# Mamba scan: the layer norm's affine moved into the weights, and one group in three with its B product on GpSimd

## The chip, the cores and the metric

The kernel runs on one core of one Trainium2 chip. A core has five engines that work side by side, each on its own queue of instructions: TensorE (PE, with its weight loads as PEld), VectorE (DVE), ScalarE (ACT), GpSimd (POOL) and SyncE (SP), which here issues the DMA transfers. The metric is the device time of one execution in microseconds, from the first to the last instruction; the time before is the median of three runs.

## The reference

Four layers follow one another on an image of shape (4, 96, 64, 64): a Mamba block with fusion (L0), an SSD block (L1), a second Mamba block (L2) and a ConvNeXt block (L3). The change is in the two Mamba blocks. Each runs two sublayers over the sequence of 4096 tokens of 96 channels, and a sublayer computes this:

```python
h = (seq - mu) * jax.lax.rsqrt(var + EPS) * ln_g + ln_b
xz = h @ in_w
xs, z = jnp.split(xz, 2, axis=-1)
xp = jnp.pad(xs, ((0, 0), (DCONV - 1, 0), (0, 0)))
xc = sum((conv_w[:, k] * xp[:, k:k + L, :] for k in range(DCONV))) + conv_b
xc = jax.nn.silu(xc)
dbl = xc @ xproj_w                      # dt: 6 columns, B: 16, C: 16
delta = jax.nn.softplus(dt @ dt_w + dt_b)
dA = jnp.exp(delta[..., None] * A)      # 192 channels x 16 states
dBx = delta[..., None] * Bm[:, :, None, :] * xc[..., None]
hstates = associative_scan(comb, (dA, dBx), axis=1)[1]   # h = dA * h + dBx along the tokens
y = jnp.einsum('blds,bls->bld', hstates, Cm) + Dp * xc
y = y * jax.nn.silu(z)
return y @ out_w
```

After the two sublayers a 1x1 fusion with batch statistics closes the block. All data are float32.

## The kernel before

**Tiling.** A Mamba block is worked off in steps. A step is one pair of images, one sublayer and one chunk of 512 tokens: 2 x 2 x 8 = 32 steps in a block, 64 in both. With 192 channels, 2 images and 16 states a step has 6144 rows to scan. The channels of both images lie in three tiles j of 128 partitions, and the rows of a step are split into 24 groups (three j, four q, two halves p). A group holds two halves of 128 partitions (8 channels by 16 states) by 512 tokens.

**The front of a step** (`mamba_front`) is a generator. It runs ahead, one step in advance, in small portions between the groups of the current step. It normalizes (PE for centering and variance, ACT for the rsqrt, DVE L184 for the product, GpSimd L185 for the affine with gain and bias), convolves with the input projection multiplied into the taps (L194), projects z (L204), then dt, B and C (L217), and computes delta with softplus (`softplus`, DVE L267 and L270, GpSimd L271) and du = delta * x (GpSimd L248). delta and du are written to DRAM as `dd` and `dg`, so that they can be read back spread over partitions; B and C go the same way into `bc`. The tuple `PACE` says how many portions of the front run in each of the 24 slots of a step, and `LEAD` = 4 how many slots earlier it starts.

**The life of a group** (`Scan.run`) is spread over several slots:

- `load`, four groups ahead: SyncE reads delta from `dd`, each of 8 rows repeated for 16 states, into a tile `da` (two transfers of 256 KB). A group marked `dma` also reads du from `dg` in this way, into a second tile of the same tag. The tag has six buffers.
- `decay`, two groups ahead: ACT turns `da` into exp(delta * A) (L107).
- `spread`, one group ahead. In an ordinary group PE spreads du over the states by a 0/1 matrix into the PSUM tile `bs` (L313). In a `dma` group ACT writes the exponentials into `bs` instead, and GpSimd multiplies the loaded du by B in place (L308).
- `scan`: in an ordinary group DVE multiplies `bs` by B (L335) and then runs two scans (L340); in a `dma` group it only runs the two scans. GpSimd multiplies the states by C into `hc` (L342, three buffers), and ACT keeps the last column for the next chunk (L345).
- `sums`, two groups later: PE adds the 16 states of each channel into the PSUM tile `py` (L361). At the end of a j, `close` multiplies by silu(z) on DVE (L369), and `project` and `fuse` bring the result back to 96 channels (L377, L381, L510 to L512).

So in every group one operand of DVE's scans lies in PSUM. Before the change a group is a `dma` group where q is even and p is 1, which is one group in four: 6 of 24.

**Order.** The program is written as one stream, and a scheduler orders each engine's queue at build time; on the chip every queue is worked off in order. A wait on one engine therefore holds up everything behind it in that queue. SyncE's queue holds all loads and all writes of `dd`, `dg` and `rows`.

**The weights** (`mamba_weights`) are prepared once per sublayer: the taps of the convolution are multiplied by the input projection, with the convolution's bias as a 97th row of the last tap, which meets a row of ones in `h`.

Of the kernel before, what the change touches and what calls it, by code (L numbers as in the profile page):

```python
# [18 lines left out]
F32 = mybir.dt.float32  # L19
AF = mybir.ActivationFunctionType  # L20
ALU = mybir.AluOpType
# [4 lines left out]
B, C, HH, WW = 4, 96, 64, 64  # L26
L = HH * WW
P = 128
T = 512
# [6 lines left out]
DIN = 192  # L36
# [8 lines left out]
NQU = QUART // HEIGHT  # L45
GS = 2
# [108 lines left out]
def mamba_front(tc, k, X, pools, wt, pair, c, h, made):  # L155

    nc = tc.nc  # L160
    work, psum, dram = pools
    if c == 0:
        nc.vector.memset(h[:C, :, 0:3], 0.0)
    else:
        nc.scalar.copy(h[:C, :, 0:3], h[:C, :, T : T + 3])

    def bank(name):
        return psum.tile([P, T], F32, tag="mm", name=name)

    for b in range(2):  # L170
        pc = bank("pc")[:C]
        nc.tensor.matmul(
            pc, lhsT=k.center, rhs=X[:, 2 * pair + b, ds(c * T, T)], start=True, stop=True
        )
        sq = work.tile([P, T], F32, tag="ua", name="sq")[:C]
        nc.scalar.activation(sq, pc, AF.Square)
        yield
        pv = bank("pv")[:C]
        nc.tensor.matmul(pv, lhsT=k.mean, rhs=sq, start=True, stop=True)
        rs = work.tile([P, T], F32, tag="lg", name="rs")[:C]  # L180
        rsqrt(k.act, rs, pv, k.eps[:C])
        yield
        dst = h[:C, b, 3 : 3 + T]
        nc.vector.tensor_tensor(dst, pc, rs, ALU.mult)  # L184
        nc.gpsimd.tensor_scalar(dst, dst, wt["ln"][:, 0:1], wt["ln"][:, 1:2], ALU.mult, ALU.add)  # L185


    xz = made["xz"] = work.tile([P, 6, T], F32, name="xz", bufs=2)
    for j in range(3):
        pu = bank("pu")  # L190
        for tap in range(4):
            kk = C + 1 if tap == 3 else C
            for r0, r1, d0, d1, b in SEGS[j]:
                nc.tensor.matmul(  # L194
                    pu[r0:r1], lhsT=wt["conv"][:kk, tap, d0:d1], rhs=h[:kk, b, ds(tap, T)],
                    start=(tap == 0), stop=(tap == 3),
                )
            yield
        nc.scalar.copy(xz[:, j], pu)
    k.act.other(xz[:, :3], xz[:, :3], AF.Silu)  # L200
    for j in range(3):
        pz = bank("pz")
        for r0, r1, d0, d1, b in SEGS[j]:
            nc.tensor.matmul(  # L204
                pz[r0:r1], lhsT=wt["in"][:, DIN + d0 : DIN + d1], rhs=h[:C, b, 3 : 3 + T],
                start=True, stop=True,
            )
        yield
        nc.scalar.copy(xz[:, 3 + j], pz)


    dbl = work.tile([P, T], F32, name="dbl")
    pd = bank("pd")
    for n in range(2):
        for b in range(2):
            j, r0, r1 = ROWS[b][n if b == 0 else 1 - n]
            nc.tensor.matmul(  # L217
                pd[2 * QUART * b : 2 * QUART * (b + 1)], lhsT=wt["xproj"][r0:r1, j],
                rhs=xz[r0:r1, j], start=(n == 0), stop=(n == 1),
            )  # L220
    yield
    nc.scalar.activation(dbl, pd, AF.Identity, bias=wt["one"])


    rows = dram.tile([P, T], F32, name="rows")
    nc.sync.dma_start(rows, dbl)
    bc = made["bc"] = work.tile([P, 2, 2, T], F32, name="bc", bufs=2)


    du = made["du"] = work.tile([P, 3, T], F32, name="du", bufs=2)  # L230
    for j in range(3):
        pt = bank("pt")
        for r0, r1, d0, d1, b in SEGS[j]:
            half = ds(HALFP * b, HALFP)
            nc.tensor.matmul(
                pt[r0:r1], lhsT=wt["dt"][half, d0:d1], rhs=dbl[half], start=True, stop=True,
            )
        delta = work.tile([P, T], F32, name="delta", bufs=2)
        softplus(nc, k.act, work, delta, pt)
        yield  # L240
        if j == 0:
            for b in range(2):
                for q in range(2):
                    r = HALFP * b + (QUART if q else RANK + 1)
                    nc.sync.dma_start(
                        bc[:, b, q], rows[r : r + NST, None].to_broadcast([NST, HEIGHT, T])
                    )
        nc.gpsimd.tensor_tensor(du[:, j], delta, xz[:, j], ALU.mult)  # L248
        for name, x in (("dd", delta), ("dg", du[:, j])):
            made[name, j] = dram.tile([P, T], F32, name=f"{name}{j}")  # L250
            nc.sync.dma_start(made[name, j], x)
    k.act.other(xz[:, 3:], xz[:, 3:], AF.Silu)

PACE = (1,) * 8 + (2,) + (1,) * 7 + (2,) + (1,) * 7
LEAD = 4


# [14 lines left out]
class Scan:  # L274
# [13 lines left out]
    def load(self, g):  # L288

        for name, which in (("da", "dd"), ("du", "dg")) if g["dma"] else (("da", "dd"),):  # L290
            g[name] = self.state.tile([P, GS, T], F32, tag="da", name=name, bufs=6)
            for i in range(GS):
                r = QUART * g["quarters"][i] + HEIGHT * g["q"]
                src = g["made"][which, g["j"]][r : r + HEIGHT].partition_broadcast(NST)
                self.tc.nc.sync.dma_start(g[name][:, i], src)
# [87 lines left out]
    def run(self, steps, wts, front, first):  # L383

        units = [(j, q, p) for j in range(3) for q in range(NQU) for p in range(2)]
        made = [first] + [{} for _ in steps[1:]]
        groups = [
            dict(
                pair=pair, sub=sub, c=c, wt=wts[sub], made=made[n], j=j, q=q, half=p, quarters=(p, p + 2),
                first=(q == 0 and p == 0), last=(q == NQU - 1 and p == 1),  # L390
                dma=(q % 2 == 0 and p == 1),
            )
            for n, (pair, sub, c) in enumerate(steps) for j, q, p in units
        ]
        total, each = len(groups), len(units)
        ahead = iter(())
        for n in range(-4, total + 6):
            slot = (n + LEAD) % each
            if slot == 0:
                for _ in ahead:  # L400
                    pass
                step = (n + LEAD) // each + 1
                ahead = front(step, made[step]) if step < len(steps) else iter(())

            def at(lag):
                return groups[n - lag] if 0 <= n - lag < total else None

            if (g := at(3)) and g["last"]:
                self.close(g)
            for stage, lag in (  # L410
                (self.load, -4), (self.spread, -1), (self.decay, -2), (self.scan, 0), (self.sums, 2),
            ):
                if g := at(lag):
                    stage(g)

            for lag, what in ((4, self.project), (5, self.fuse)):
                if (g := at(lag)) and g["last"] and g["j"] and (g["sub"] or lag == 4):
                    what(g, g["j"] - 1)
            for _ in range(PACE[slot] if slot < len(PACE) else 0):
                next(ahead, None)  # L420


def mamba_weights(nc, act, ident, wpool, w, sub, one7):
    wt = {"one": one7}

    def load(name, shape):
        wt[name] = wpool.tile(shape, F32, name=f"w_{name}{sub}")
        nc.sync.dma_start(wt[name], w[name][sub])

    load("ln", [C, 2])  # L430
    load("in", [C, 2 * DIN])
    conv = wt["conv"] = wpool.tile([C + 1, 4, DIN], F32, name=f"w_conv{sub}")
    nc.sync.dma_start(conv[:C], w["conv_wT"][sub].partition_broadcast(C))
    nc.sync.dma_start(conv[C : C + 1, 3], w["conv_b"][sub : sub + 1])
    nc.vector.tensor_tensor(
        conv[:C], conv[:C], wt["in"][:, None, :DIN].to_broadcast([C, 4, DIN]), ALU.mult
    )
    xp = wt["xproj"] = wpool.tile([P, 3, 2 * QUART], F32, name=f"w_xproj{sub}")
    nc.vector.memset(xp, 0.0)
    nb = RANK + 1 + NST  # L440
# [26 lines left out]
def mamba_fusion(ctx: ExitStack, tc, k, src, dst, w):  # L467

    nc = tc.nc
    one = ctx.enter_context(tc.tile_pool(name="m1", bufs=1))  # L470
# [5 lines left out]
    psum = ctx.enter_context(tc.tile_pool(name="mps", bufs=2, space=PSUM))  # L476
    dram = ctx.enter_context(tc.tile_pool(name="mdram", bufs=3, space=DRAM))

    one7 = one.tile([P, 1], F32, name="one7")
# [6 lines left out]
    h = one.tile([C + 1, 2, T + 3], F32, name="h")  # L486
# [25 lines left out]
        nc.vector.bn_stats(stats[:, b * NT + c], xs)  # L512
        nc.sync.dma_start(dst[b, :, ds(c * T, T)], xs)

    wts = [mamba_weights(nc, k.act, k.ident, one, w, 0, one7)]
    carry = one.tile([P, 3, P // HEIGHT], F32, name="carry")
    steps = [(pair, sub, c) for pair in range(B // 2) for sub in range(2) for c in range(NT)]

# [10 lines left out]
    for n, _ in enumerate(front(0, made)):  # L529
        if n % 4 == 3 and n // 4 - 1 in range(B):  # L530
            b = n // 4 - 1
            nc.vector.reduce_sum(gsum[:, b : b + 1], X[:, b], axis=AX.X)
    wts.append(mamba_weights(nc, k.act, k.ident, one, w, 1, one7))

    gpw = one.tile([C, C], F32, name="gpw")
    nc.sync.dma_start(gpw, w["gp_wT"])
# [752 lines left out]
```

## Time and profile before

| | |
|---|---|
| time, median of three | 10031.32 us (10020.4 to 10053.84) |
| profiled execution | 10010.64 us, span 10008.9 us |
| DVE, POOL, PE, ACT busy in the span | 82%, 70%, 86%, 55% |
| first to last scan of Mamba block L0 | 77 to 3044 us |
| granted TensorE clock | 0.939 of full speed on average |
| q1, the DMA queue of SyncE | 1520 MB, 54.6% of 16 engines' span |

A line of the view of groups reads: line of the kernel, engine, operation, output <- inputs with shapes, number of instructions, then busy time in us and mean ns of one, then the idle time of the engine just before them and what ended it. A line of the waits view reads: the waiting engine and instruction, what it waited for, then us in total, number of waits, longest. A line of the timeline gives start and duration in us. The windows view gives for a stretch its length, each engine's busy time and number of instructions, and then the TensorE clock, the share of time in which the 16 DMA engines were busy, and GB/s.

### The profile page before, as it was taken

How to read it: one execution, taken by the hardware profiler on the slowest of the kernel's cores; microseconds unless marked ns; L12 is line 12 of the kernel's file. 1: busy time of each engine (PE TensorE's matmuls, PEld its weight loads, DVE VectorE, ACT ScalarE, POOL GpSimd, SP SyncE). 2: the span in 40 equal slices, each digit the busy share in tenths (PEclk: the TensorE clock that was granted, in tenths of full speed). 3: DMA queues.
4: the chain of work that ended last, by engine and by line, in shares of the span. 5: the costliest groups of instructions: out<-in, count | busy, mean ns of one | idle time of the engine just before them, and what ended most of it. 6: DMA issues, size and time to landing. Idle time of an engine off the chain costs nothing. (4 is left out here: it accounts for less than half of the span.)

```text
span 10008.9 us, 110272 instructions
## 1 busy us (share of the span) xinstructions
PE 8562.4 (86%) x33120; PEld 3566.0 (36%) x33120; DVE 8200.6 (82%) x10877; ACT 5497.9 (55%) x10460; POOL 6966.5 (70%) x4600
## 2 busy tenths in 40 slices
PE   7888888888886888888888888788888888887688
PEld 1222212222214766666776676122222222221122
DVE  7999999999994666667666666799999999999787
ACT  5566666656653445445445444566666665665244
POOL 6888888888883555555555555688888888888322
PEclk9999999999997999999999999899999999999798
DMA  7777777777773223223222221777777767777442
GB/s 190 200 205 204 201 206 207 201 201 209 204 197 105 72 66 94 65 66 95 72 66 74 81 64 51 188 201 204 210 200 203 208 196 204 207 204 199 113 99 73
DMA packets 802257, 1527.53 MB, mean 153 GB/s; under 512 B 123933, under 2 KB 127161, under 8 KB 800890
## 3 DMA queue, kind: packets, MB, share of 16 engines
q1 hardware_dynamic: 801658, 1520.47, 54.6%
q8 instruction: 263, 4.31, 0.2%
q14 instruction: 336, 2.75, 0.1%
HBM read 1229.30 MB, written 155.98 MB: 138 GB/s over the span
## 5 line engine op out<-in xcount | busy, mean ns | idle before, releaser
L342 POOL TENSOR_TENSOR hc<-hs,bc 128x1024 f32<-128x1024 f32 x1536 | 3608.0, 2355 | 622.2 <-DVE hs L340 554.8
L340 DVE TENSOR_TENSOR_SCAN hs<-da,carry,bs 128x512 f32<-128x512 f32 x2016 | 2466.4, 1264 | 79.2 <-POOL du L308 1.0
L107 ACT ACTIVATE da<-da,w_a 128x512 f32<-128x512 f32 x2304 | 1616.5, 716 | 1268.5 <-DMA da<-dd 1218.7
L361 PE MATMUL py<-hc,selsum 128*32 128x512 f32 x6144 | 1801.4, 638 | 462.5 <-POOL hc L342 448.3
L313 PE MATMUL bs<-du,seldu 64*128 64x512 f32 x4608 | 1573.3, 676 | 204.2 <-DVE hs L340 194.5
L335 DVE TENSOR_TENSOR bs<-bs,bc 128x1024 f32<-128x1024 f32 x1152 | 1397.7, 1213 | 184.0 <-PE bs L313 181.6
L308 POOL TENSOR_TENSOR du<-du,bc 128x1024 f32<-128x1024 f32 x384 | 904.5, 2355 | 281.3 <-DMA du<-dg 160.5
L863 POOL TENSOR_TENSOR seg<-seg,cb 128x384 f32<-128x384 f32 x512 | 514.7, 1006 | 818.1 <-DVE cb L862 750.0
L361 PEld LDWEIGHTS py<-hc,selsum 128*32 128x32 f32 x6144 | 240.6, 110 | 1815.1 <-POOL hc L342 1118.2
L313 PEld LDWEIGHTS bs<-du,seldu 64*128 64x128 f32 x4608 | 446.0, 195 | 1196.2 <-DVE hs L340 852.1
L848 DVE TENSOR_SCALAR seg<-dr,dac 128x128 f32<-128x128 f32 x1536 | 660.4, 458 | 256.9 <-PE y L892 249.3
L194 PE MATMUL pu<-h,w_conv 96*128 96x512 f32 (+3 forms) x2048 | 834.6, 629 | 6.5 <-ACT rs L107 6.3
L340 DVE TENSOR_TENSOR_SCAN hs<-bs,carry,du 128x512 f32<-128x512 f32 x672 | 823.5, 1260 | 7.8 <-issue 5.0
L799 PE MATMUL front<-pk,sconv 128*128 128x512 f32 x1536 | 767.9, 609 | 9.2 <-ACT z L787 5.1
L915 ACT ACTIVATE y<-yz 128x192 f32<-128x192 f32 x512 | 186.0, 363 | 919.3 <-DVE yz L914 918.3
L867 POOL TENSOR_TENSOR xs<-pre,coef 128x576 f32<-128x576 f32 x512 | 598.3, 1175 | 56.2 <-ACT pre L112 31.5
L810 PE MATMUL front<-sconv,pk 128*128 128x192 f32 x3072 | 577.2, 330 | 45.3 <-DVE pre L815 36.0
L1152 DVE SCALAR_TENSOR_TENSOR acc<-pad,c_conv,acc 96x1024 f32<-96x1024 f32 x336 | 491.9, 1468 | 109.1 <-ACT acc L1143 58.0
L902 POOL TENSOR_TENSOR y<-y,xs 128x192 f32<-128x192 f32 x496 | 293.5, 592 | 412.8 <-DVE y L901 412.1
L345 ACT COPY carry<-hs 128x2 f32<-128x2 f32 x1344 | 250.7, 187 | 564.2 <-DVE hs L340 560.4
L107 ACT ACTIVATE bs<-da,w_a 128x512 f32<-128x512 f32 x768 | 522.0, 680 | 2.5 <-DMA da<-dd 0.7
L810 PEld LDWEIGHTS front<-sconv,pk 128*128 128x128 f32 x3072 | 497.4, 191 | 69.3 <-DVE pre L815 57.7
(191 smaller groups left out, 13881.2 us busy)
## 6 DMA issues: line engine op xcount, KB each, us to landing
da<-dd SPq DMA_DIRECT2D x3072, 256.0 KB
du<-dg SPq DMA_DIRECT2D x768, 256.0 KB
dr<-rows SPq DMA_DIRECT2D x256, 384.0 KB
bc<-rows SPq DMA_DIRECT2D x256, 256.0 KB
dd<-delta SPq DMA_DIRECT2D x192, 256.0 KB
dg<-du SPq DMA_DIRECT2D x192, 256.0 KB
pk<-xn SPq DMA_DIRECT2D x128, 384.0 KB
pk<-xn SPq DMA_DIRECT2D x128, 256.0 KB
```

Source lines behind the costliest of these rows:

```text
L107: self.last = self.scalar.activation(out, in_, func, **kw)
L194: nc.tensor.matmul(pu[r0:r1], lhsT=wt["conv"][:kk, tap, d0:d1], rhs=h[:kk, b, ds(tap, T)], start=(tap == 0), stop=(tap == 3),)
L308: nc.gpsimd.tensor_tensor(g["du"], g["du"], self.b_or_c(g, 0), ALU.mult)
L313: nc.tensor.matmul(g["bs"][:, i], lhsT=self.sel["du"][rows, g["half"], g["q"]], rhs=g["made"]["du"][rows, g["j"]], start=True, stop=True,)
L335: nc.vector.tensor_tensor(dbx, dbx, self.b_or_c(g, 0), ALU.mult)
L340: nc.vector.tensor_tensor_scan(hs[:, i], da[:, i], dbx[:, i], init, ALU.mult, ALU.add)
L342: nc.gpsimd.tensor_tensor(g["hc"], hs, self.b_or_c(g, 1), ALU.mult)
L361: nc.tensor.matmul(py[rows], lhsT=self.sel["sum"][:, g["q"]], rhs=g["hc"][:, i], start=(g["q"] == 0), stop=(g["q"] == NQU - 1),)
L799: nc.tensor.matmul(p, lhsT=self.conv[:, i, DI + q * DST : DI + (q + 1) * DST], rhs=pk[:, i, ds(c * T, T)], start=(i == 0), stop=(i == 2),)
L810: nc.tensor.matmul(p, lhsT=pk[:, i, ds(c * Q, Q)], rhs=self.conv[:, i, :DI], start=(i == 0), stop=(i == 2),)
L848: nc.vector.tensor_scalar(seg[:, h], g["pair"]["dr"][:, c % 2 * NH + h], made["dac"][:, n0 + h : n0 + h + 1], 0.0, ALU.subtract, ALU.min,)
L867: nc.gpsimd.tensor_tensor(xs, x.to_broadcast([P, 3, NH, HD]), coef.to_broadcast([P, 3, NH, HD]), ALU.mult)
```

## The change

It has three parts that belong together.

First, the affine of the layer norm is folded into the weights. The gain multiplies the rows of the convolution's and z's weights. The bias becomes a 97th row of every tap and of z: a small matmul of a matrix `shift`, whose last column is the layer norm's bias, with the weights gives this row at the start. `h` has a row of ones, which now is part of every matmul; it is zeroed, like the channels, in the three columns of padding before the first token. GpSimd's L185 is no longer needed.

Second, the groups whose index in the step is 1 modulo 3 are `dma` groups, 8 of 24. In these du comes by DMA and its product with B is on GpSimd, not on PE and DVE. The tag `da` gets seven buffers in place of six.

Third, `PACE` runs one portion of the front in each of the 24 slots. It had two portions in slots 8 and 16, so that the front was through two slots before the step's end.

```diff
     if c == 0:
-        nc.vector.memset(h[:C, :, 0:3], 0.0)
+        nc.vector.memset(h[:, :, 0:3], 0.0)
     else:
-        nc.scalar.copy(h[:C, :, 0:3], h[:C, :, T : T + 3])
+        nc.scalar.copy(h[:, :, 0:3], h[:, :, T : T + 3])
...
-        dst = h[:C, b, 3 : 3 + T]
-        nc.vector.tensor_tensor(dst, pc, rs, ALU.mult)
-        nc.gpsimd.tensor_scalar(dst, dst, wt["ln"][:, 0:1], wt["ln"][:, 1:2], ALU.mult, ALU.add)
+        nc.vector.tensor_tensor(h[:C, b, 3 : 3 + T], pc, rs, ALU.mult)
...
-            kk = C + 1 if tap == 3 else C
             for r0, r1, d0, d1, b in SEGS[j]:
                 nc.tensor.matmul(
-                    pu[r0:r1], lhsT=wt["conv"][:kk, tap, d0:d1], rhs=h[:kk, b, ds(tap, T)],
+                    pu[r0:r1], lhsT=wt["conv"][:, tap, d0:d1], rhs=h[:, b, ds(tap, T)],
...
-                pz[r0:r1], lhsT=wt["in"][:, DIN + d0 : DIN + d1], rhs=h[:C, b, 3 : 3 + T],
+                pz[r0:r1], lhsT=wt["z"][:, d0:d1], rhs=h[:, b, 3 : 3 + T],
...
-PACE = (1,) * 8 + (2,) + (1,) * 7 + (2,) + (1,) * 7
+PACE = (1,) * 24
...
-            g[name] = self.state.tile([P, GS, T], F32, tag="da", name=name, bufs=6)
+            g[name] = self.state.tile([P, GS, T], F32, tag="da", name=name, bufs=7)
...
-                dma=(q % 2 == 0 and p == 1),
+                dma=((j * NQU + q) * 2 + p) % 3 == 1,
...
-    load("in", [C, 2 * DIN])
-    conv = wt["conv"] = wpool.tile([C + 1, 4, DIN], F32, name=f"w_conv{sub}")
+    both = wpool.tile([C + 1, 5, DIN], F32, name=f"w_conv{sub}")
+    conv, z = wt["conv"], wt["z"] = both[:, :4], both[:, 4]
     nc.sync.dma_start(conv[:C], w["conv_wT"][sub].partition_broadcast(C))
-    nc.sync.dma_start(conv[C : C + 1, 3], w["conv_b"][sub : sub + 1])
+    nc.sync.dma_start(z[:C], w["in"][sub, :, DIN:])
+    wx = wpool.tile([C + 1, DIN], F32, name="w_x")
+    nc.sync.dma_start(wx[:C], w["in"][sub, :, :DIN])
+    nc.sync.dma_start(wx[C:], w["conv_b"][sub : sub + 1])
     nc.vector.tensor_tensor(
-        conv[:C], conv[:C], wt["in"][:, None, :DIN].to_broadcast([C, 4, DIN]), ALU.mult
+        conv[:C], conv[:C], wx[:C, None].to_broadcast([C, 4, DIN]), ALU.mult
     )
+    shift = wpool.tile([C, C + 1], F32, name="w_shift")
+    nc.vector.memset(shift, 0.0)
+    nc.vector.tensor_copy(shift[:, C:], wt["ln"][:, 1:2])
+    for n in range(0, 5, 2):
+        m = min(2, 5 - n)
+        ps = psum.tile([P, T], F32, tag="mm", name="ps")[: C + 1, : m * DIN]
+        nc.tensor.matmul(ps, lhsT=shift, rhs=both[:C, n : n + m], start=True, stop=True)
+        nc.scalar.copy(both[C:, n : n + m].rearrange("p k n -> p (k n)"), ps[C:])
+    nc.vector.tensor_tensor(conv[C:, 3], conv[C:, 3], wx[C:], ALU.add)
+    nc.vector.tensor_scalar_mul(both[:C], both[:C], wt["ln"][:, 0:1])
```

## The prediction

> **What bounds the kernel now.** I read the page first (part 1, busy shares), then cut the span by stage with the windows view, then took the groups of instructions, the waits and the timeline of the stage that the change touches. The two Mamba layers run from 77 to 3049 us (first scan to the last of layer L0) and from 6337 to 9304 us; between and behind them lie the SSD and ConvNeXt layers, which the diff does not touch.
>
> ```profile
> core 0: us, PE busy (x) PEld busy (x) DVE busy (x) ACT busy (x) POOL busy (x), PEclk, DMA share, GB/s
> 77.00:3049.00 2972.00, 2585.65 (x7863) 597.75 (x7862) 2761.99 (x2552) 1817.91 (x3258) 2523.23 (x1208) 0.95 0.72 202
> 6290.00:9294.00 3004.00, 2582.84 (x7872) 599.13 (x7870) 2770.10 (x2557) 1837.97 (x3285) 2521.30 (x1210) 0.95 0.73 202
> ```
>
> VectorE (DVE) is busy 2762 of 2972 us, 93%; GpSimd (POOL) 85%; ACT 61%; the DMA engines 72%. PE shows 87%. A layer is 32 steps (2 pairs, 2 sublayers, 8 chunks) of 24 groups, so one step takes 2972 / 32 = 92.9 us.
>
> ```profile
> L340 DVE TENSOR_TENSOR_SCAN hs<-da,carry,bs 128x512 f32<-128x512 f32 x1008 | 1233.2, 1264 | 40.7 <-POOL du L308 1.0 <-DVE bs L335 0.9 <-ACT carry L345 0.5
> L335 DVE TENSOR_TENSOR bs<-bs,bc 128x1024 f32<-128x1024 f32 x575 | 697.7, 1213 | 95.1 <-PE bs L313 94.1
> L340 DVE TENSOR_TENSOR_SCAN hs<-bs,carry,du 128x512 f32<-128x512 f32 x336 | 411.7, 1260 | 4.0 <-issue 2.3 <-POOL hc L342 1.1 <-ACT bs L107 0.4
> ...
> L342 POOL TENSOR_TENSOR hc<-hs,bc 128x1024 f32<-128x1024 f32 x768 | 1804.1, 2356 | 304.1 <-DVE hs L340 267.9 <-PE py L361 23.8 <-issue 6.8
> L308 POOL TENSOR_TENSOR du<-du,bc 128x1024 f32<-128x1024 f32 x192 | 452.2, 2355 | 144.9 <-DMA du<-dg 86.1 <-DMA da<-dd 19.3 <-PE pd L217 14.3
> L248 POOL TENSOR_TENSOR du<-delta,xz 128x512 f32<-128x512 f32 x93 | 117.9, 1268 | 7.3
> L271 POOL TENSOR_TENSOR delta<-delta,lg 128x512 f32<-128x512 f32 x93 | 117.8, 1267 | 0.1
> L185 POOL TENSOR_SCALAR h<-h,w_ln 96x512 f32<-96x512 f32 x62 | 47.6, 768 | 0.5 <-DVE h L184 0.5
> ```
>
> The reader is to see two kinds of group. In an ordinary group DVE multiplies by B (L335) and scans twice; in a "dma" group (one in four) GpSimd does that product (L308) and DVE only scans. DVE hardly waits before scans; it waits before L335, for PE's spread. The timeline gives what a group really costs on DVE, start to start:
>
> ```profile
> 1011.84 1.22 DVE L335 TENSOR_TENSOR bs<-bs,bc 128x1024 f32<-128x1024 f32 x1
> 1013.16 2.45 DVE L340 TENSOR_TENSOR_SCAN hs<-da,carry,bs 128x512 f32<-128x512 f32 x2
> 1015.53 1.21 DVE L335 TENSOR_TENSOR bs<-bs,bc 128x1024 f32<-128x1024 f32 x1
> ...
> 1023.31 2.43 DVE L340 TENSOR_TENSOR_SCAN hs<-bs,carry,du 128x512 f32<-128x512 f32 x2
> 1025.66 0.67 DVE L512 BATCH_NORM_STATS2 stats<-X 96x6 f32<-96x512 f32 x1
> ```
>
> An ordinary group is 1015.53 - 1011.84 = 3.69 us (the scan starts 0.10 after the product ends), a dma group 1025.66 - 1023.31 = 2.35. The short instructions of the front take about 0.59 each (1063.90 to 1064.50, 1020.35 to 1020.95). A step has about 14 of them: 6 of softplus, 3 closes, 2 of the layer norm, 2 residual adds, 1 statistic on average. So a step is 18 x 3.69 + 6 x 2.35 + 14 x 0.59 = 66.4 + 14.1 + 8.3 = 88.8 us of DVE, and 4.1 us of waiting. The waits view of the stage:
>
> ```profile
> DVE bs L335 <- PE bs L313: 94.1, 77, 4.1
> DVE lg L270 <- ACT pt L268: 18.9, 31, 2.0
> DVE h L184 <- ACT rs L107: 17.0, 18, 2.9
> DVE xz L369 <- PE py L361: 14.3, 5, 4.0
> ```
>
> **What the Trainium skill says.** "Trace Analysis", section Identifying the Most-Contended Engine: occupancy is a fair measure for Vector and GpSimd, matmul occupancy is not. The trace agrees: PE's 87% does not stop DVE from being 93% busy. "SBUF — State Buffer", section SBUF: two separate sides: DVE and GpSimd share a port pair, and one shuts out the other only where DVE has two SBUF inputs or a two-port mode. Both kinds of scan, and L335, read one operand from PSUM, so more GpSimd work should not stretch DVE: here scans take 1264 and 1260 ns, and GpSimd's product 2355 beside both. "GPSIMD Engine Reference", section 3.1: some 2.6 cycles an element for a two-input product, an estimate of 2.2 us for 1024 elements; the trace has 2.355, which I use.
>
> **The change, part by part.** (1) Groups with index mod 3 equal to 1 take the dma path: 8 of 24 instead of 6. Two groups a step turn from 3.69 to 2.35 us on DVE: 2 x 1.34 = 2.7 us off the engine that bounds the step, 64 steps: 172 us. PE loses their spread (four rows, 1.13 us a group in the timeline, 2.3 us a step), on an engine that DVE waits for.
> (2) On GpSimd the same two groups add 2 x 2.34 = 4.7 us (a pair runs in 4.68), and L185, the layer norm's affine, goes: 2 x 0.77 = 1.5 us. Its work rises from 30 x 2.34 + 6 x 1.27 + 1.5 = 79.3 to 32 x 2.34 + 7.6 = 82.5 us a step. DVE falls from 88.8 to 86.1. So GpSimd still has the smaller sum, but the gap shrinks from 9.5 to 3.6 us: 96% of DVE's work instead of 89%. Inside a run of three groups DVE needs 2 x 3.69 + 2.35 = 9.73, GpSimd 4 x 2.34 = 9.36.
> (3) Does that queue hurt? GpSimd runs in order, so a du product delays the hc products behind it; PE's sums (L361) wait for hc, and PE's next spread stands behind those, for which DVE waits at L335. In the order in which the changed kernel's instructions are written out, du of group g mostly stands behind hc of g-4 or g-3 (223 of 256 in a layer), as before (191 of 192). Following three steady groups by hand from the end of scan g-5: hc(g-4) can start at 3.7 and ends at 6.0; du(g) is done at 8.4; scan g is due at about 13.5, so it does not wait. Around the softplus GpSimd has 3 x 2.53 us more and DVE 6 x 0.59 more: it falls back some 4 us, of which du and the three hs buffers take up most. I add 0.4 us of wait a step; the bounds are 0 and 3.
> (4) Loads: 4 more of 256 KB a step on some 72, DMA share 0.72 to about 0.78 at the shorter step. The "da" buffers go from 6 for 30 tiles a step (4.8 groups ahead) to 7 for 32 (5.25 ahead). GpSimd's wait for du<-dg was 86.1 us in the layer, 2.7 a step, for data it was early for; ACT waited 608 us for da with DVE hardly waiting for ACT. I cost the loads at nothing: scans three to five groups long hide them.
> (5) PACE becomes flat: 24 turns of the front instead of 26. In the written order the first delta of the next step is finished after scan 20 instead of 17. Its dd write stands in SyncE's queue ahead of the next step's da loads; behind it, ACT's exps and the scans of the next step wait. From scan 20 to the next step's first scan are three groups and four short instructions, about 12 us; the products, the write and the read take about 8 (1.3 + 1.3 on GpSimd, the rest an estimate from du loads, which land some 6 us after their buffer comes free). Hidden, by a margin of one group. The same reordering puts silu(z) on ACT where 5 us of DVE work cover it, so the 2 us wait of L270 may go; I leave that out.
> (6) The affine in the weights: DVE's L184, the conv matmuls and their count stay; 97 rows instead of 96 cost nothing (x644 against x618 ns in the two forms of before, mixed by waits). The extra weight work comes before each layer's first scan: one more load in SyncE's queue, three matmuls, three ACT copies and two DVE products, some 3 us per layer (estimate: 0.6 for a load as in SyncE's timeline, 1 for 97x960 by L435's 0.95, 1.5 for matmul and copy ahead of the layer norm): +6 us.
> Sum: 64 x (2.7 - 0.4) = 147 off, 6 on: 10031 - 141 = 9890 us.
>
> **Rivals.** A: as summed, 9890. B: GpSimd becomes the co-bound. For it: 96% of DVE's work, and its own waits for other engines than DVE need not vanish (144.9 before L308 and 23.8 for PE before hc: 5.3 us a step); 82.5 + 5.3 + half of the 8.4 us (267.9 / 32) that it waited for DVE = 92.0 a step, 0.9 less than now: 10031 - 58 + 6 = 9979. Against it: the waits for du were early ones. C: slower. The step's end is late: delta comes three groups later, GpSimd works without a pause there, SyncE waits in order for dd and dg of each j; if the next step's first dma group misses by 5 us, a step takes 90.2 + 5 = 95.2: 10031 + 147 + 6 = 10184. For it: SyncE already waits 232.9 us for delta. Against: the margin above. D: more than DVE's saving, since PE has 2.3 us less and L270's wait (2) and half of the waits for PE go: 86.1 + 2 a step, 64 x 4.8 = 307 off, 6 on: 9730.
>
> **How the numbers follow.** A 0.57, B 0.20, C 0.13, D 0.10. Predicted 9890, the value of A. Low 9790 takes in A without the added wait (9865) and part of D; high 10030 holds B and no change, and leaves C out. Faster by over 0.3% (under 10001) is A, D and most of B: 0.81; within 0.3% is the rest of B and a weak C: 0.07; slower 0.12.
>
> **What would show it.** Right: x256 du products and x512 L335 in a layer, L185 gone, GpSimd at about 91% of a stage of some 2900 us, DVE's scans still near 1260 ns, DVE's waits near 5 us a step. Wrong: a new wait of DVE's scans on POOL du or of L335 on PE with PE waiting for hc (B), scans waiting for ACT da or DMA at each step's start (C), the SSD stage changed, or a DVE instruction stretched beside GpSimd.

## The result, and the profile after

The changed kernel takes 10337.65 us (10334.9 to 10341.4), the kernel before beside it 10025.86: a ratio of 1.0307, 95% interval [1.0285, 1.0329]. It is slower by 312 us, where 9890 us and a range of 9790 to 10030 were forecast.

The windows view of the changed kernel over its first Mamba block (its last scans now end at 3188 us, not 3044), with the columns of the same view above. Lines of the softplus and of the scan have numbers lower by three than in the kernel before.

```profile
core 0: us, PE busy (x) PEld busy (x) DVE busy (x) ACT busy (x) POOL busy (x), PEclk, DMA share, GB/s
77.00:3200.00 3123.00, 2671.78 (x7616) 602.73 (x7616) 2692.87 (x2491) 1794.76 (x3230) 2616.54 (x1210) 0.91 0.77 203
```

DVE's work fell as forecast: 2692.87 us in place of 2761.99, 69 us a block or 2.2 a step. What grew is its idle time: 3123 - 2693 = 430 us against 2972 - 2762 = 210, which is 13.4 us a step against 6.6. The balance, 6.9 - 2.2 = 4.7 us a step, is 301 us in 64 steps, nearly the whole loss. GpSimd's 2617 us of work are 84% of the longer block, so it has idle time in total. The groups of the page:

```profile
L332 DVE TENSOR_TENSOR bs<-bs,bc 128x1024 f32<-128x1024 f32 x1024 | 1239.8, 1216 | 532.6 <-PE bs L310 528.6
L337 DVE TENSOR_TENSOR_SCAN hs<-bs,carry,du 128x512 f32<-128x512 f32 x896 | 1091.9, 1259 | 2.2 <-issue 1.6
L358 PE MATMUL py<-hc,selsum 128*32 128x512 f32 x6144 | 1814.8, 648 | 724.1 <-POOL hc L339 715.5
L305 POOL TENSOR_TENSOR du<-du,bc 128x1024 f32<-128x1024 f32 x512 | 1208.7, 2361 | 170.0 <-DMA du<-dg 98.1
```

The scans of dma groups wait for nothing (2.2 us in the whole run), so du comes in time. The waits are in two places: DVE before its product with B (L335 before, L332 now), for PE's spread, and PE before the sums (L361, now L358), for GpSimd's hc. The waits view of the block, from 85 to 3190 us, and behind it PE's line of the kernel before, from 77 to 3049 us:

```profile
PE py L358 <- POOL hc L339: 356.4, 252, 7.9
DVE bs L332 <- PE bs L310: 254.8, 117, 7.2
DVE delta L264 <- ACT lg L107: 68.1, 43, 3.7
```

```profile
PE py L361 <- POOL hc L342: 222.7, 271, 4.1
```

DVE waited 94.1 us for the spread before, with a longest wait of 4.1 us. Where in a step this falls, two stretches of one step tell, its middle and its end with the beginning of the next:

```profile
1066.00:1108.00 42.00, 38.38 (x124) 8.48 (x122) 41.08 (x37) 24.14 (x46) 36.30 (x17) 1.00 0.74 197
1108.00:1166.00 58.00, 49.41 (x113) 10.76 (x112) 42.31 (x43) 33.35 (x60) 43.83 (x22) 0.77 0.72 194
```

In the middle DVE is busy for 41.08 of 42 us at a full TensorE clock. At the end it is busy for 42.31 of 58, and the clock is 0.77. The timelines of GpSimd, PE and DVE there (start, duration, and in brackets the idle time just before):

```profile
1141.51 1.27 POOL L268 TENSOR_TENSOR delta<-delta,lg 128x512 f32<-128x512 f32 x1 [2.02 <-DVE lg L267]
1142.85 1.27 POOL L245 TENSOR_TENSOR du<-delta,xz 128x512 f32<-128x512 f32 x1
1144.08 2.35 POOL L305 TENSOR_TENSOR du<-du,bc 128x1024 f32<-128x1024 f32 x1
1146.39 6.95 POOL L339 TENSOR_TENSOR hc<-hs,bc 128x1024 f32<-128x1024 f32 x3
1153.31 2.35 POOL L305 TENSOR_TENSOR du<-du,bc 128x1024 f32<-128x1024 f32 x1
1162.68 2.35 POOL L339 TENSOR_TENSOR hc<-hs,bc 128x1024 f32<-128x1024 f32 x1 [7.02 <-DVE hs L337]
```

```profile
1143.36 1.10 PE L179 MATMUL pv<-sq,mean 96*96 96x512 f32 x2
1144.39 1.05 PE L358 MATMUL py<-hc,selsum 128*32 128x512 f32 x2
1148.78 1.61 PE L358 MATMUL py<-hc,selsum 128*32 128x512 f32 x4 [3.35 <-POOL hc L339]
1150.32 2.02 PE L172 MATMUL pc<-X,center 96*96 96x512 f32 x2
1152.27 2.07 PE L310 MATMUL bs<-du,seldu 64*128 64x512 f32 x2
1154.28 2.02 PE L179 MATMUL pv<-sq,mean 96*96 96x512 f32 x2
1156.23 2.08 PE L310 MATMUL bs<-du,seldu 64*128 64x512 f32 x4
```

```profile
1158.34 1.23 DVE L332 TENSOR_TENSOR bs<-bs,bc 128x1024 f32<-128x1024 f32 x1 [7.21 <-PE bs L310]
```

Read it as a chain (pc and pv are the next layer norm's matmuls, for centering and variance). The softplus's add and product, and a du product, stand ahead of three hc products on GpSimd: the first of these starts 4.9 us after L268 began. PE waits 3.35 us for it. Then a pair of pv matmuls, which took 1.10 us before the wait, takes 2.02: the granted clock has fallen to half. The spread stands behind pc and pv in PE's queue, all at half rate, and DVE waits 7.21 us for it. That starves GpSimd in turn: at 1162.68 it has waited 7.02 us for DVE's scans, and time that it was short of is lost. This is one stretch; the table at the end of the experiments shows where DVE waits over the whole block.

### The profile page after: what moved, and what is told of

It reads as the page before. It is cut to its first block, busy times and chain, and to the rows that moved or that the text cites. A ratio compares the mean times of both kernels' runs of the same rounds, so it can differ in the third digit from the quotient of the medians.

```text
span 10339.7 us, 110448 instructions
## 1 busy us (share of the span) xinstructions
PE 8794.5 (85%) x32632; PEld 3592.5 (35%) x32632; DVE 8068.6 (78%) x10765; ACT 5454.1 (53%) x10410; POOL 7155.6 (69%) x4600
## 4 chain that ended last, share of the span: by engine, by line
PE 26%; DVE 20%; POOL 9%; issue 6%; ACT 3%; DMA 3%; SPq 1%; POOLq 0%; DVEq 0%; another core or an unknown queue 0%; ACTq 0%
DVE hs L337 7%; PE front L811 5%; POOL hc L339 4%; PE front L822 3%; DVE seg L860 2%; DVE bs L332 2%; PE y L904 2%; PE py L358 2%; DVE yz L926 2%; PE bs L310 2%; PE out L953 2%; POOL du L305 2%; DMA du<-dg 2%; DVE acc L1164 2%; PE dw L1151 1%
## 5 line engine op out<-in xcount | busy, mean ns | idle before, releaser
L358 PE MATMUL py<-hc,selsum 128*32 128x512 f32 x6144 | 1814.8, 648 | 724.1 <-POOL hc L339 715.5
L337 DVE TENSOR_TENSOR_SCAN hs<-da,carry,bs 128x512 f32<-128x512 f32 x1792 | 2199.1, 1265 | 72.2 <-DVE bs L332 1.4
L107 ACT ACTIVATE da<-da,w_a 128x512 f32<-128x512 f32 x2048 | 1427.6, 715 | 590.0 <-DMA da<-dd 552.7
L332 DVE TENSOR_TENSOR bs<-bs,bc 128x1024 f32<-128x1024 f32 x1024 | 1239.8, 1216 | 532.6 <-PE bs L310 528.6
L310 PE MATMUL bs<-du,seldu 64*128 64x512 f32 x4096 | 1409.2, 691 | 96.1 <-DVE hs L337 89.3
L305 POOL TENSOR_TENSOR du<-du,bc 128x1024 f32<-128x1024 f32 x512 | 1208.7, 2361 | 170.0 <-DMA du<-dg 98.1
L337 DVE TENSOR_TENSOR_SCAN hs<-bs,carry,du 128x512 f32<-128x512 f32 x896 | 1091.9, 1259 | 2.2 <-issue 1.6
L358 PEld LDWEIGHTS py<-hc,selsum 128*32 128x32 f32 x6144 | 241.2, 111 | 2065.1 <-POOL hc L339 1343.4
L191 PE MATMUL pu<-h,w_conv 97*64 97x512 f32 (+1 forms) x2048 | 906.3, 638 | 2.2 <-ACT rs L107 1.5
L310 PEld LDWEIGHTS bs<-du,seldu 64*128 64x128 f32 x4096 | 393.1, 201 | 1079.0 <-DVE hs L337 531.3
L107 ACT ACTIVATE bs<-da,w_a 128x512 f32<-128x512 f32 x1024 | 699.8, 683 | 106.9 <-DVE hs L337 97.7
```

Source lines behind the costliest of these rows:

```text
L107: self.last = self.scalar.activation(out, in_, func, **kw)
L191: nc.tensor.matmul(pu[r0:r1], lhsT=wt["conv"][:, tap, d0:d1], rhs=h[:, b, ds(tap, T)], start=(tap == 0), stop=(tap == 3),)
L305: nc.gpsimd.tensor_tensor(g["du"], g["du"], self.b_or_c(g, 0), ALU.mult)
L310: nc.tensor.matmul(g["bs"][:, i], lhsT=self.sel["du"][rows, g["half"], g["q"]], rhs=g["made"]["du"][rows, g["j"]], start=True, stop=True,)
L332: nc.vector.tensor_tensor(dbx, dbx, self.b_or_c(g, 0), ALU.mult)
L337: nc.vector.tensor_tensor_scan(hs[:, i], da[:, i], dbx[:, i], init, ALU.mult, ALU.add)
```

## The experiments

All ratios are to the kernel before, run beside each kernel on the same chip; 95% intervals in brackets. Differences in us are between medians. The median of the kernel before moved between 10009 and 10026 us from one set of runs to the next, so a difference between kernels of different sets is good to some 20 us.

**The parts of the change.** First each part alone and two together, to find the one that costs. The fold alone (the diff above without its other two parts):

> Before with only the affine folded into the weights (old dma groups, six buffers, old PACE). GpSimd has 1.5 us less a step and the norm one hop less. Both theories: within 0.5% of before; a third, that the 97-row matmuls or the weights' preparation cost the time: over 10200 us.

Measured: 10046.39 us, 1.0032 [1.0016, 1.0048]. The fold costs 0.3%. The flat PACE alone:

```diff
-PACE = (1,) * 8 + (2,) + (1,) * 7 + (2,) + (1,) * 7
+PACE = (1,) * 24
```

> Before with nothing but the flat PACE. Theory G: within 0.5% of before. Theory P: slower, 10150 to 10350 us, with DVE's waits in the stretch from the softplus to the second layer norm of a step.

Measured: 10345.66, 1.0325 [1.031, 1.0341]. This one line costs as much as the whole change, though GpSimd's work stays what it was (2523.67 us a block against 2523.23 before). DVE's longest waits in its block, from 77 to 3220 us:

```profile
DVE bs L335 <- PE bs L313: 157.8, 46, 5.5
DVE delta L267 <- ACT lg L107: 107.5, 54, 3.8
```

The thirds alone, with the old PACE (two small tiles of the fusion share one allocation so that the seventh buffer fits):

```diff
-            g[name] = self.state.tile([P, GS, T], F32, tag="da", name=name, bufs=6)
+            g[name] = self.state.tile([P, GS, T], F32, tag="da", name=name, bufs=7)
...
-                dma=(q % 2 == 0 and p == 1),
+                dma=((j * NQU + q) * 2 + p) % 3 == 1,
...
```

> Before, with the dma groups at index 1 modulo 3 and seven da buffers, the old PACE and the old layer norm with L185 (two small tiles share one allocation, so that the seventh buffer fits). Theory G (GpSimd's extra products delay hc, PE's sums and with them PE's spread): slow already, 10200 to 10400 us, L335's wait for PE 200 us or more in a layer. Theory P (the flat PACE puts the softplus and the next layer norm of the front into the same stretch at the step's end, and PE's queue blocks there): faster than before, 9880 to 9950, with L335's wait near 94 us.

Measured: 10662.99, 1.0642 [1.0624, 1.066]. Fold and thirds with the old PACE, which is the changed kernel with that one line put back:

> The changed kernel with the old PACE (two portions of the front in slots 8 and 16). Theory G: as slow as the changed kernel, 10300 or more. Theory P: faster than before, 9860 to 9950 us. If both parts are needed for the loss: between 9950 and 10200.

Measured: 10650.31, 1.0628 [1.0613, 1.0644]. Fold and flat PACE without the thirds:

> Before with the fold and the flat PACE, old dma groups, six buffers. If the flat PACE is what costs: 10300 to 10400, as with the PACE alone. If the fold repairs it (no hop over GpSimd in the norm): below 10100.

Measured: 10369.31, 1.0358 [1.0342, 1.0373]. So neither G nor P of these expectations holds alone. The thirds and the flat PACE each cost by themselves, and do not add up: the flat PACE costs 3% with one group in four and saves 3% with one in three (10650 to 10338).

**The order of TensorE's queue.** The theory called Q was that the scheduler's order on PE, with pc and pv ahead of the spread, is the cause. All Mamba matmuls are chained in the order of the program:

```diff
+        ins = self.tc.nc.tensor.matmul(*args, **kw)
+        if self.last is not None:
+            order = mybir.DependencyInfo(mybir.DependencyClass.NoSync, mybir.DependencyReason.DATA)
+            self.tc.add_manual_dep(ins.ins, self.last.ins.name, order, reason="in order")
+        self.last = ins
...
-        nc.tensor.matmul(
+        k.pe.matmul(
...
```

> The changed kernel, with the Mamba matmuls held on TensorE in the order in which the program names them (spread of the next group, then the sums, then the front), no work or wait changed otherwise. Theory Q (in the queue as scheduled, spreads stand behind sums whose hc is late and behind the front's pc and pv, and TensorE's clock drops after each such wait): below 9950 us, L332's wait for PE below 95 us in a layer, granted clock 0.93 or more. Theory G (GpSimd is simply too loaded with 8 of 24 products, whatever the order): above 10150, PE's wait for hc still over 300 us.

> The kernel before with the same order on TensorE. Theory Q: 9850 to 10020, a little faster than before, since before has the same pattern once a step; and the in-order changed kernel is then faster than this one by 2.7 us a step, some 170. Theory G: within 0.5% of before.

Measured: changed kernel 10410.36, 1.0402 [1.0386, 1.0417]; kernel before 10248.16, 1.0237 [1.022, 1.0255]. Q fell: with that order PE waits for the layer norm and the softplus instead (154.7 us for sq and 139.4 for lg in the changed kernel between 600 and 2900 us). G, as it is put there, did not come out either: PE's wait for hc in that stretch fell from 240.7 to 89.3 us and the time did not, and the kernel before lost 2.4% by the same order.

**Is it TensorE's work?** Two theories were left: T, that TensorE cannot catch up after a wait, and G, that GpSimd is late and TensorE only hands this on. The sums in bfloat16 (they are rounded then) take most of TensorE's largest item away (1801 to 688 us in the kernel before):

```diff
-        g["hc"] = self.state.tile([P, GS, T], F32, name="hc", bufs=3)
+        g["hc"] = self.state.tile([P, GS, T], BF16, name="hc", bufs=3)
...
-        "sum": one.tile([P, NQU, QUART], F32, name="selsum"),
+        "sum": one.tile([P, NQU, QUART], BF16, name="selsum"),
```

> The changed kernel with the states' products hc and the matrix selsum in bfloat16, so that the sums L358 are bfloat16 matmuls (the sums are rounded; nothing else is changed). Theory T (TensorE cannot catch up: its queue is in order, its clock drops after each wait, and the sums are two thirds of its work): TensorE's busy time in a Mamba block falls from 2693 to some 1300 us, DVE's wait for the spread (254.8 us) nearly goes, and the time is 9850 to 9960. Theory G (GpSimd is late with hc around the softplus, and TensorE only hands this on): PE still waits for hc, DVE still waits over 150 us for the spread in a block, and the time is 10200 to 10340.

> The kernel before with the same two tiles in bfloat16: the control for the run above. Theory T: the wait of DVE for the spread (94.1 us in a block) goes, and little else: 9830 to 9900, so that the change on top of it is worth about what my sum gave (0 to 2% faster). Theory G: 9950 to 10030, and the change on top of it still costs 2 to 3%.

Measured: changed kernel 10459.31, 1.0446 [1.0421, 1.0472]; kernel before 10251.01, 1.0238 [1.0217, 1.026]. Both are slower with less to do, which neither theory had; between the two the change still costs 2.0%, as G had it. The first expectation starts from a wrong number: 2693 us is DVE's busy time, PE's is 2672, of which the sums are 903, a third and not two thirds. With them in bfloat16 the changed kernel's PE is still busy for 2477 of 3123 us. The windows of the kernel before with these sums, and its groups:

```profile
77.00:3050.00 2973.00, 2412.94 (x6166) 689.28 (x6167) 2664.16 (x2463) 1785.33 (x3192) 2433.48 (x1169) 0.81 0.68 196
```

```profile
L313 PE MATMUL bs<-du,seldu 64*128 64x512 f32 x4608 | 1822.1, 808 | 219.1 <-DVE hs L340 213.8
L361 PE MATMUL py<-hc,selsum 128*32 128x512 bf16 x3072 | 688.2, 447 | 899.9 <-POOL hc L342 894.8
```

TensorE waits twice as long for hc (894.8 us in the whole run, 448.3 before), its clock in the block falls from 0.95 to 0.81, and the spread, which was not touched, takes 808 ns instead of 676. The scheduler also writes the queues anew for these sums, so the run does not price the clock; it shows a lower rate together with longer waits.

**GpSimd's add in the softplus.** L268 is 3 x 1.27 us a step, all at the step's end (beside groups 20 to 23 and the next step's first, counted from 0). Left out (the correction is computed but not added, so delta is a little off):

```diff
-    nc.gpsimd.tensor_tensor(out, out, t, ALU.add)
+    pass
```

> The changed kernel without GpSimd's add L268 in the softplus (its correction term is computed and not added, so delta is a little off): 3 x 1.27 = 3.8 us less of GpSimd's work in a step, all of it around the step's end, and delta is ready earlier. Theory G: GpSimd's lateness there is what DVE pays for, so 3 to 5 us a step come back: 10010 to 10150. Theory T: GpSimd was not the cause, and under 80 us come back: 10260 to 10340.

> The kernel before without GpSimd's add in the softplus (computed and not added, delta a little off): the control for the same edit in the changed kernel, which gave 330 us. If the loss comes from GpSimd's load around the softplus together with the denser products there, the kernel before has the slack for it and gains less than 60 us: 9960 to 10030. If the add delays every kernel's step (delta later, then its loads), it gains 150 us or more: below 9870.

Measured: changed kernel 10005.66, 0.999 [0.9981, 0.9998], 332 us less than with the add; kernel before 9920.79, 0.9903 [0.9887, 0.9919], 95 us less. The same 3.8 us of GpSimd's work cost 5.2 us a step in the changed kernel and 1.5 in the kernel before (95 us lies between the two expectations, under 60 and 150 or more). The waits and the windows of the changed kernel without it:

```profile
DVE bs L332 <- PE bs L310: 86.2, 83, 3.9
PE py L358 <- POOL hc L339: 176.8, 205, 3.3
```

```profile
77.00:3050.00 2973.00, 2558.17 (x7616) 578.65 (x7616) 2687.97 (x2503) 1808.03 (x3233) 2502.68 (x1118) 0.95 0.78 214
```

PE's wait for hc halves, DVE's wait for the spread falls to a third, and the clock is 0.95 again. With the add on DVE nothing is left out:

```diff
-    nc.gpsimd.tensor_tensor(out, out, t, ALU.add)
+    nc.vector.tensor_tensor(out, out, t, ALU.add)
```

> The changed kernel with the softplus's last add on DVE instead of GpSimd, nothing left out. GpSimd loses 3.8 us a step as in the run that left the add out, DVE gains 3 x 0.6 = 1.8 us a step. If GpSimd's load at the step's end is what is paid for: the 10006 of that run plus 64 x 1.8 = 115, so 10080 to 10160. If the run that left it out gained because delta was ready earlier rather than because GpSimd was free, about the same; if DVE stretches beside GpSimd on two SBUF operands, more. If neither: about 10340 + 115.

Measured: 10132.95, 1.0121 [1.0104, 1.0137], 205 us less than the changed kernel. The expected number came out, with DVE paying for the add. One reserve: in these two variants of the changed kernel PE's queue is ordered anew in places (without the add, po stands some nine entries earlier in a steady step, by the traces), while the kernel before keeps its order on PE all but exactly. So the add's price in the changed kernel holds some of that too.

**Where the eight products stand.** First other residues, then eight groups away from the softplus, then only six:

```diff
-dma=((j * NQU + q) * 2 + p) % 3 == 1,
+dma=((j * NQU + q) * 2 + p) % 3 == 0,
...
+dma=((j * NQU + q) * 2 + p) in (2, 4, 6, 8, 11, 13, 15, 17),
...
+dma=((j * NQU + q) * 2 + p) in (1, 4, 7, 10, 13, 16),
```

> The changed kernel with the groups of index 0 modulo 3, not 1, on the DMA path: eight as before, the same work on every engine, other neighbours of the softplus. If the sums of work per engine (GpSimd at 96% of DVE) cause the loss, the time is within 50 us of 10338. If it is where the products stand against the softplus at the step's end (Theory G) it differs by more than 100 us, either way.

> The changed kernel with its eight groups of a step at 2, 4, 6, 8, 11, 13, 15 and 17 in place of 1, 4, 7, ... 22: the same work on every engine, none of it between the group 18 and the next step's group 1, where the softplus stands. If it is the placement (GpSimd over its share around the softplus), the loss goes and the sums of the forecast come true: 9850 to 10000. If it is the sum over a step (GpSimd at 96% of DVE), or if GpSimd is now over its share at the alternating groups: 10250 to 10400.

> The changed kernel with six groups of a step on the DMA path, 1, 4, 7, 10, 13 and 16, none from 17 to 24: the same sums on every engine as in the run with the fold and the flat PACE (10369.31, groups 1, 5, 9, 13, 17, 21), only placed away from the softplus. Placement: GpSimd has two products less beside the softplus than the changed kernel, and the loss of 3% goes: 9980 to 10120. Sum, or flat PACE by itself: 10300 to 10400, as that run.

Measured: residue 0 gives 10315.91, 1.0299 [1.0275, 1.0324]; eight away 10496.04, 1.0477 [1.0455, 1.05]; six early 10242.41, 1.0212 [1.0184, 1.0241]. The phase hardly matters for the time (22 us), but it moves the wait: with residue 0 DVE waits 116.6 us for the spread from 77 to 3049 us, little more than the 94.1 of the kernel before, and instead waits for ACT's part of the softplus (77.2 us before L267 alone). So the way through PE to the spread is one way by which the step's end costs DVE its time, not the only one. Eight away made it worse, beyond its expectation: where a dma group and an ordinary one alternate, GpSimd needs 3 x 2.34 = 7.0 us for two groups and DVE 3.69 + 2.35 = 6.0, so the overload went elsewhere, as the table below shows. Six early is 127 us below six evenly spread (10369.31; that run has six buffers, this one seven), about half of the least that "placement" expected. So placement is a part, not the whole.

**Idle matmuls.** Two matmuls of zeros per group ahead of the last four groups' sums, for TensorE to run while it waits:

```diff
+        if g["j"] == 2 and g["q"] > 1:
+            zero, some = self.sel["du"][:QUART, 1, g["q"], :QUART], self.sel["du"][:QUART, 0]
+            for i in range(GS):
+                nc.tensor.matmul(
+                    py[ds(QUART * g["quarters"][i], QUART)], lhsT=zero, rhs=some,
+                    start=False, stop=False,
+                )
```

> The changed kernel with two more matmuls of zeros (they add 0 to py) ahead of the sums of the last four groups of a step, which TensorE can run while it waits for hc: eight more matmuls of some 0.5 us. If the clock that falls in such a wait, and the half rate of the matmuls behind it, is a cause of its own, the wait is filled, the spread behind it comes at full rate, and the time falls by 60 to 250 us: 10090 to 10280. If TensorE is only handing on GpSimd's delay, or its queue is too full to take more, the time stays or rises: 10330 to 10500.

> The kernel before with the eight matmuls of zeros a step that gave the changed kernel 132 us. If the clock is a cause of its own in both kernels, 20 to 60 us come back here too (granted clock 0.94, waits for the spread 94.1 us a block): 9960 to 10000. If the clock matters only where GpSimd makes TensorE wait long, nothing or a small loss: 10010 to 10060.

> The kernel of e16 with the matmuls of zeros too. If placement has taken away the long waits, the idle matmuls add nothing: within 40 us of e16. If the fall of the clock is a second cause, 50 to 130 us less than e16, and then the fastest of all with nothing left out: below 9980.

Measured: changed kernel 10205.67, 1.0186 [1.0171, 1.0201], 132 us less; kernel before 10137.12, 1.0119 [1.0104, 1.0134], 117 us more; six early 10163.31, 1.0135 [1.0113, 1.0158], 79 us less. The windows of the changed kernel with them:

```profile
77.00:3150.00 3073.00, 2708.22 (x8126) 603.44 (x8126) 2693.34 (x2501) 1794.39 (x3231) 2616.05 (x1211) 0.95 0.78 207
```

DVE and GpSimd do the same work as in the changed kernel, TensorE has eight matmuls a step more, and the block is some 50 us shorter, at a clock of 0.95 in place of 0.91. By the trace's record of the granted clock, TensorE stood at half rate for 557 us of the changed kernel's block, and for 330 us with the idle matmuls (294 in the kernel before). Steps 4 to 25 of the traces have the same order on DVE and GpSimd, and on PE, the added matmuls aside, about one sum a step stands elsewhere. So the gain is not one of a new order: the fall of the clock is a cause of its own where TensorE waits long. In the kernel before it seldom does (12 waits of 1.75 us or more before the sums in the block, 75 in the changed kernel), and there the added matmuls only cost. Six early stayed far from the 9980 that its expectation had for a second cause.

No kernel that leaves nothing out beat the kernel before.

**Where in the step DVE waits.** DVE's idle time in the first block, in us a step, by the group of the step (counted from 0) ahead of whose scans it falls; worked out from the traces:

| kernel | groups 0-2 | 3-16 | 17-23 | all |
|---|---|---|---|---|
| before | 1.4 | 3.1 | 1.9 | 6.4 |
| changed | 4.7 | 2.4 | 5.9 | 13.0 |
| flat PACE alone | 0.6 | 1.6 | 9.6 | 11.8 |
| changed, residue 0 | 0.5 | 4.0 | 7.9 | 12.4 |
| changed, eight away | 3.0 | 12.4 | 0.8 | 16.2 |
| changed, six early | 5.6 | 2.6 | 1.7 | 9.9 |
| changed, no add | 3.6 | 2.1 | 2.7 | 8.4 |
| changed, idle matmuls | 3.6 | 1.7 | 6.3 | 11.5 |
| thirds alone | 1.1 | 7.9 | 10.0 | 19.1 |

All of the idle time that the change added lies between group 17 and the next step's group 2; groups 3 to 16 wait even less than before. The flat PACE alone loses its time in groups 19 to 21 (9.3 us a step), half of it in waits for the spread at group 21. Eight away empties the step's end and fills the alternating stretch (4.3 us at group 12 alone).

## Why the prediction was wrong

- **(1) right.** DVE's work fell by 2.2 us a step, where 2.7 was forecast start to start; scans still take 1259 and 1265 ns.
- **(2) right as a sum.** GpSimd's work is 2617 us a block, 81.8 a step (82.5 forecast). The inference that the smaller sum leaves it harmless was wrong; and the flat PACE alone, which leaves that sum as it was, cost as much.
- **(3) the step that failed:** "I add 0.4 us of wait a step; the bounds are 0 and 3". DVE's idle time grew by 6.9. I followed du to the scan, and there I was right: DVE's scans do not wait for it. I did not follow hc on through PE to the next spread, though the same paragraph names that way. GpSimd's falling back by "some 4 us" around the softplus was to be taken up by three hs buffers; instead it came out as PE's wait for hc, and the 332 us for an add of 3.8 us a step against 95 in the kernel before show that this slack was used up. What I had no term for is that PE then works at half rate; with the waits filled 132 us came back.
- **(4) right.** ACT's wait for da fell from 608 to 272 us, and GpSimd's for du<-dg from 86.1 to 47.7.
- **(5) failed too:** "Hidden, by a margin of one group". The flat PACE alone costs 3.2%. The margin that I worked out was for dd's way through DRAM, and DVE's scans hardly waited for it (3.9 us for da in the block with the flat PACE alone). What the later softplus costs shows as DVE's waits for ACT's part of the softplus and for the spread at the step's end (9.3 us a step in groups 19 to 21 with the flat PACE alone).
- **(6) too small.** The fold alone costs 26 us (10046.39 against 10019.95 of the kernel before in the same runs), not 6. The setup of the first layer cost what was forecast: its first scan starts 3 us later, at 80.1 us. Most of the rest lies in the steps: each block is 21 to 23 us longer in that run's trace (of 10069.67 us), with the same work on DVE and more idle time. What it waits for there stays open.
- **The rivals.** B named the sign that came (L335 on PE, PE waiting for hc), C the place (the step's end) and that the kernel gets slower. Neither had the size: each let one engine be late once a step, where here one engine's lateness slows the next, and the starved one loses time that it needs.

Four things stay open: why the thirds cost so much with the old PACE (6.4%), why without the add the changed kernel is still 85 us behind the kernel before without it, whether the flat PACE's loss with six groups would go with the add too (no run shows it), and how much of each run is the queue that the scheduler writes anew after every edit.

## What to carry to other kernels

Where in-order engines hand work round in a ring, the difference of their sums over a step is no margin (the flat PACE alone lost 3% at unchanged sums): look for the stretch in which short extra work meets the regular load, and follow its delay through every queue of the ring to the bounding engine. Take a little work off the suspect, in both kernels: if the same edit gives several times more in one, its slack is gone there. And before work is moved off the bounding engine, ask whether the engine that receives it feeds TensorE, since a wait of TensorE can cost again in its rate.

## What the runs showed of the hardware

TensorE's clock falls to half after shorter waits than expected. The Trainium skill, "TensorE: Matmul & The Clock Gate", section HAM oscillation, gives idle gaps of more than about 3.4 us as the limit. Here the waits of TensorE that began at full clock, between 300 and 2900 us, were set against the trace's record of the granted clock: a fall to half during the wait or within 1 us of its end.

| wait | changed kernel | kernel before |
|---|---|---|
| 0.25 to 1.75 us | 3 of 136 | 18 of 331 |
| 1.75 to 2.5 us | 5 of 29 | 8 of 9 |
| 2.5 to 3.41 us | 18 of 19 | 2 of 2 |
| longer | 10 of 10 | 2 of 2 |

So waits of 2.5 us and more were nearly always followed by half rate, and shorter ones in part. The length of one wait is not all that counts: in the kernel before, 21 of the 34 falls of that stretch came with no wait of 1.75 us or more in the 3.4 us before. The first case of the stretch above is a short one:

```profile
1124.43 1.10 PE L522 MATMUL pf<-X,fus 96*96 96x512 f32 x2
1125.46 1.05 PE L358 MATMUL py<-hc,selsum 128*32 128x512 f32 x4
1128.53 1.93 PE L374 MATMUL po<-xz,w_out 64*96 64x512 f32 x2 [2.02 <-ACT X L523]
```

Here the clock fell at the end of a wait of 2.02 us: the pair of po takes 1.93 us, and 1.10 at full clock (at 1234.96 us). The measurement decides over the page's limit. And with less work for TensorE both kernels were slower: with the sums in bfloat16 the clock in the block is 0.81 in the kernel before, and the float32 spread beside them takes 808 ns in place of 676, though the queues differ too.
